# Small and large pieces of an attention batch put into halves over two steps, in a fused attention and Hadamard feed-forward kernel

## Chip, cores and metric

The kernel runs on one core of a Trainium2 chip. The metric is the device time of one execution in microseconds, lower being better. Three runs of the kernel before gave 2101.51, 2101.54 and 2102.27 us; the median is 2101.54 us.

## What is computed

Eight batches of 512 rows with 512 features, all float32. Attention has 16 heads of 32 features. Keys come from the row itself, queries and values from a compression to 128 features. Both are rotated (rotary embedding). Its output goes through an output projection and a layer norm and is added to the input; then a feed-forward block does the same with Hadamard transforms around its weights.

```python
x = layernorm(x_in)
c_kv = x @ W_dkv + b_dkv;  c_q = x @ W_dq + b_dq          # 512 -> 128
v = c_kv @ W_uv + b_uv                                     # 128 -> 512
q = rotary(c_q @ W_qr + b_qr);  k = rotary(x @ W_kr + b_kr)
attn = softmax(q @ k.T / sqrt(32)) @ v                     # 16 heads
x1 = x_in + layernorm(attn @ W_o + b_o)
h = fwht(layernorm(x1) * SU_ug) / 64
h = silu(h @ W_gate.T * s_g) * (h @ W_up.T * s_u)          # 512 -> 2048
out = x1 + layernorm((fwht(h * SU_dp) / 64) @ W_down.T * s_d)
```

The second Hadamard transform is applied to the down weights instead of the data ("fold"): its 16 parts are worked off during attention.

## The kernel before

**Two halves.** Attention takes the first 923 us or so, the feed-forward block the rest. The change touches attention alone.

**Steps.** Attention is one loop of 128 steps, written out by hand: the engines get their instructions in just the order of the program text, each engine its own queue. A batch has 4 groups of 4 heads, a group 4 steps (one for each 128 keys). Step "b.i" below is step i (0 to 15) of batch b; c is i modulo 4. Every step has the same core on TensorE (PE):

- `scores_t` (L564, L573): transposed scores t of 4 heads, first the rows' maxima as a bias in bf16, then k against q. They go to two PSUM tiles of two banks each, from a pool "s" of three.
- `weigh` (L606, "ops"): the weights of the step before times v.
- `row_max` (L527, "s"): scores of a group six steps ahead, into two more tiles of pool "s", from which VectorE (DVE) takes the maxima (L535, "nm").

So in a step pool "s" hands out t, t, s, s in turn. The second t of a step takes the tile that the first s of the step before had: it waits for DVE's first `nm`. The second s takes the first t's: it waits for ScalarE's (ACT) first exponential (L585, "p").

Some steps have more of it: at c = 2 the sums of the weights ("l", L623); at c = 3 the transposes of the maxima ("ps_b", L550), whose input GpSimd (POOL) makes by splitting the maxima into three bf16 parts (`split`, L543 to L545), issued two steps earlier, at c = 1. At c = 3 the second exponential stands behind the copy of ps_b (L554) in ACT's queue.

**Add-ups.** At c = 1 and c = 3 POOL adds two steps' weights (`add_up`, L594, four instructions, in place, so it must wait for `weigh`). At the next c = 0 DVE adds the two results (`add_pairs`, L599, two instructions), behind that step's `nm` in its queue.

**Pieces.** Everything else that attention needs is cut into pieces that stand in the steps. Large ones have four 512-column matmuls: `key` (L439), `compress` ("cq" and "ckv", L407), `out_proj` (L662). Small ones have one: `query` (L454), `value` (L466), `fold` (L485). `x_flip` (L394, "xt") is four transposes. Tables `BETWEEN` and `BEHIND` say which piece stands in which step: BETWEEN ahead of `row_max` (or, for steps in `TWO`, ahead of the BEHIND piece, with a tile of pool "s"), BEHIND at the end of the step. Pieces other than those of TWO use the one bank "f", which ACT must have emptied before the next one writes to it. In batches 1 to 5 the steps hold: 0 value and xt; 1 key and xt; 2 query; 3 value; 4 fold and xt; 5 compress; 6 key; 7 to 10 the four output projections, with a query at 8 and 9 and a fold at 10; 11 key; 12 query and compress; 13 value and xt; 14 key; 15 value.

**Behind a piece.** A key or a query leaves PSUM through ACT; its rotation follows (`rotate`): a shuffle on DVE (L420) and three POOL instructions (L421 to L423). Rotations wait in a list, `turns`; `turn()`, called twice in a step (ahead of `weigh` and behind `row_max`), issues all that wait. A fold is followed by four levels of adds on DVE (L493, L494, one level per step) and a store. x's row statistics, its normalization on ACT, its loads and the output's statistics stand in `early` and `later`, in steps of their own.

Of the kernel before, what the change touches and what calls it, by code (L numbers as in the profile page):

```python
# [10 lines left out]
F32 = mybir.dt.float32  # L11
BF16 = mybir.dt.bfloat16
I32 = mybir.dt.int32
AF = mybir.ActivationFunctionType
# [3 lines left out]
P = 128  # L18
NB, S, D = 8, 512, 512
DH, GH = 32, 4  # L20
NK = D // P
NT = S // P
# [11 lines left out]
def sandwich_kernel(  # L34
# [142 lines left out]
    def in_step(j, had, n):  # L177

        if had:
            in_had(j)  # L180
            if j + 2 < n:
                in_shift(j + 2)
            return
        in_flip(j)
        if j + 3 < n:
            in_load(j + 3)
        if j + 1 < n:
            in_norm(j + 1)
        if j + 2 < n:
            in_stats(j + 2)  # L190
# [51 lines left out]
    with ExitStack() as actx:  # L242
# [19 lines left out]
        def load_x(b, by=1):  # L262
            xs[b] = xpool.tile([P, NT, D], F32, tag="x", name=f"x{b}")
            xv = x[b].rearrange("(c p) d -> p c d", p=P)
            for c in range(0, NT, by):
                nc.sync.dma_start(out=xs[b][:, c : c + by, :], in_=xv[:, c : c + by, :])

        def load_row(b, t):

            if b < NB - 1:  # L270
                xr[b, t] = row.tile([P, D], F32, tag="xr", name=f"xr_{b}_{t}", bufs=2)
            else:
                xr[b, t] = fo.tile(
                    [P, D], F32, tag="wwza"[t], name=f"xr_{b}_{t}", bufs=2 - t // 2
                )
            nc.sync.dma_start(out=xr[b, t], in_=x[b, ts(t, P), :])

# [100 lines left out]
        def x_shift(b):  # L378
            mv, rs = stats[b]
            stats[b] = rs, shift_of(mv, rs, NT, f"x{b}")  # L380

        def x_norm(b, t):
            rs, sh = stats[b]
            xn[b, t] = row.tile([P, D], F32, tag="xn", name=f"xn_{b}_{t}", bufs=3)
            nc.scalar.activation(
                xn[b, t], xs[b][:, t, :], AF.Identity, bias=sh[:, t : t + 1], scale=rs[:, t : t + 1]
            )
# [26 lines left out]
        def rotate(dst, ps, bias, scale, name, first=None, second=None):  # L414
            lin = rp.tile([P, S], F32, tag="lin", name=f"lin_{name}")
            nc.scalar.activation(lin, ps, AF.Identity, bias=bias, scale=scale)

            def rest():
                rot = rp.tile([P, S], F32, tag="rot", name=f"rot_{name}", bufs=2)
                nc.vector.stream_shuffle(rot, lin, swap)  # L420
                (first or nc.gpsimd).tensor_mul(lin, lin, cs[:, 0, :])  # L421
                (second or nc.gpsimd).tensor_mul(rot, rot, cs[:, 1, :])
                (first or nc.gpsimd).tensor_add(dst, lin, rot)  # L423

            turns.append(rest)

        turns = []

        def turn():

            while turns:
                turns.pop(0)()

        def key(b, g, wide=False):
            if g == 0:
# [43 lines left out]
            )  # L479
            folds.append((n, w))  # L480

        def fold(n, wide=False):
            _, w = folds.pop(0)
            ps = bank(wide, f"fd_{n}").rearrange("p (c m) -> p c m", c=NI)
            nc.tensor.matmul(ps, lhsT=h128, rhs=w, start=True, stop=True)  # L485
            z = fo.tile([P, NI, NF], F32, tag="z", name=f"fz_{n}")
            a = fo.tile([P, NI, NF], F32, tag="a", name=f"fa_{n}")
            nc.scalar.copy(z, ps)

            def level(src, dst, h):  # L490
                sv = src.rearrange("p (a t b) n -> p a t (b n)", t=2, b=h)
                dv = dst.rearrange("p (a t b) n -> p a t (b n)", t=2, b=h)
                nc.vector.tensor_add(dv[:, :, 0, :], sv[:, :, 0, :], sv[:, :, 1, :])  # L493
                nc.vector.tensor_sub(dv[:, :, 1, :], sv[:, :, 0, :], sv[:, :, 1, :])  # L494

            def keep():
                nc.sync.dma_start(
                    out=wdd.rearrange("p (c m) -> p c m", c=NI)[:, :, ts(n, NF)], in_=w
                )

            levels.extend(
                [
                    lambda: level(z, a, 1),
                    lambda: level(a, z, 2),
                    lambda: level(z, a, 4),
                    lambda: level(a, w, 8),
                    keep,
                ]
            )

        levels = []


        brow, nms, pt, o_ps, o_sb, rec = {}, {}, {}, {}, {}, {}
# [245 lines left out]
        for t in range(3):  # L760
# [10 lines left out]

        BETWEEN = {
            0: (x_flip, 1, 1), 1: (x_flip, 1, 2), 4: (x_flip, 1, 3),
            8: (query, 1, 0), 9: (query, 1, 1), 12: (query, 1, 2), 13: (x_flip, 2, 0),
        }
        BEHIND = {
            0: (value, 0, 2), 1: (key, 0, 3), 2: (query, 0, 3), 3: (value, 0, 3),
            5: (compress, 1, "cq"), 6: (key, 1, 0), 7: (out_proj, -1, 0),  # L780
            8: (out_proj, -1, 1), 9: (out_proj, -1, 2), 10: (out_proj, -1, 3),
            11: (key, 1, 1), 12: (compress, 1, "ckv"), 13: (value, 1, 0), 14: (key, 1, 2),
            15: (value, 1, 1),
        }

        FIRST_BETWEEN = {i: p for i, p in BETWEEN.items() if i not in (8, 9)}
        FIRST_BEHIND = {
            **BEHIND, 7: (query, 1, 0), 8: (None, NB, None), 9: (key, 1, 1),
            10: (None, NB, None), 11: (query, 1, 1),
        }  # L790
        OUT = {7: 0, 8: 1, 9: 2, 10: 3}

        APART = {n: (0, 2) for n in range(NG - NK, NG - 2)}
        APART[NG - 2], APART[NG - 1] = (0, 2, 3), (0, 1, 2, 3)

        FOLDS = [4, 10, 15] + [NK * NT * b + i for b in range(1, NB - 1) for i in (4, 10)]
        FOLDS.append(NK * NT * (NB - 1) + 1)
        READ = [0] + [g - 3 for g in FOLDS[1:]]


        TWO = (8, 9, 10, 12, 15)

        def piece(table, b, i, wide=False):
            if b == 0 and table is BEHIND and i == 8:
                out_bias()
            pieces = table if b else FIRST_BETWEEN if table is BETWEEN else FIRST_BEHIND
            if i in pieces:
                fn, d, what = pieces[i]
                if 0 <= b + d < NB:
                    fn(b + d, what, *([True] if wide else []))  # L810
            at = NK * NT * b + i
            if at in FOLDS and (table is BETWEEN) == (b > 0 and i in TWO or i == 15 or b == NB - 1):
                fold(FOLDS.index(at), wide)
            if b == NB - 1 and (i, table is BEHIND) in ENTRY:
                in_step(*ENTRY[i, table is BEHIND], 2 * NT)

        places = [
            (0, False), (4, False), (4, True), (5, True), (6, True), (8, False), (10, False),  # L820
            (11, True), (12, False), (12, True), (13, True), (14, True), (15, True),
        ]
        ENTRY = {place: divmod(s, 2) for s, place in enumerate(places)}
        room["xin"] = lambda name: row.tile([P, D], F32, tag="xn", name=name, bufs=3)
# [9 lines left out]
        def early(b, i):  # L834

            if b > 0 and i - 3 in OUT:
                residual(b - 1, OUT[i - 3])
            if b + 2 < NB and i in (12, 14, 15):
                x_norm(b + 2, max(i - 13, 0))
            if i == 0 and 0 < b + 1 < NB:  # L840
                x_norm(b + 1, 3)

        def later(b, i):

            if b > 0 and i - 1 in OUT:
                out_stats(b - 1, OUT[i - 1])
            if b > 0 and i - 2 in OUT:
                out_shift(b - 1, OUT[i - 2])
            if b > 0 and i - 5 in OUT:
                store(b - 1, OUT[i - 5])  # L850
            if b + 2 < NB:
                if i == 4:
                    load_x(b + 2, NT)
                elif 6 <= i < 10:
                    x_stats(b + 2, i - 6)
                elif i == 11:
                    x_shift(b + 2)

        for t in range(NG * NT):
            n, c = divmod(t, NT)  # L860
# [4 lines left out]
            ends_group = c == NT - 1 and n + 1 < NG  # L865
            if not ends_group:
                second()
            turn()
            if c == 0 and n > 1:
                invert(n - 2)  # L870
            if c == 3 and n > 1:
                divide(n - 2)
            last_steps = t + AHEAD >= NG * NT
            if last_steps:
                piece(BETWEEN, b, i)
            if t > 0:
                weigh(*divmod(t - 1, NT))
            if ends_group:
# [6 lines left out]
                    sums(n - 1, APART[n - 1])  # L885
            elif c == 2 and n > 0:
                sums(n - 1)
            if not last_steps and (i not in TWO or b == NB - 1):
                piece(BETWEEN, b, i)
            if c == 0 and n > 0:  # L890
                weighed(n - 1)
            u = t + AHEAD
# [2 lines left out]
                if u % NT == NT - 1:  # L895
                    split(u // NT)
            early(b, i)
            turn()
            if c == 0 and 0 < n <= NG - NK:
                add_pairs(n - 1)  # L900
            later(b, i)
            if b == 0 and i == 6:
                out_bias_in()
            if levels and (c > 0 or 0 < i and b < 1):
                levels.pop(0)()
            if small:
                small.pop(0)()
            if t in READ:
                fold_load(READ.index(t))
# [14 lines left out]
                load_row(b, i - 12)  # L924
            elif b == NB - 1 and i in (8, 10):
                combine(*units[i // 2 - 4][1:])
            if i in TWO and b < NB - 1:
                piece(BETWEEN, b, i, True)
            piece(BEHIND, b, i)
            if n == NG - 1 and c == 2:  # L930
                invert(NG - 2)

# [682 lines left out]
```

## Time and profile before

| what | us |
|---|---|
| median of three runs | 2101.54 |
| the profiled execution | 2102.66 |
| its span, first to last instruction | 2100.9 |
| PE busy | 2076.8 |
| POOL busy | 1575.4 |
| DVE busy | 1414.4 |
| ACT busy | 745.3 |
| attention's batch 0 (46.78 to 148.89) | 102.11 |
| batch 4 (474.86 to 583.52) | 108.66 |
| first to last of batch 7's steps 0 to 14 (800.28 to 890.50) | 90.22 |

A step begins where the first bias matmul of `scores_t` starts (L564); times are counted from the span's start. A float32 matmul of one instruction in the program is two records in the trace: "x8" of a 512-column key are its four matmuls. In the timeline a row is a run of equal instructions with its start and the time to the end of its last one; as the next run starts before the last has drained, what a run costs is read from start to start. Granted clock was 1.00 in all stretches of attention.

### The profile page before, as it was taken

The numbers are of one execution on the slowest core, as the hardware profiler recorded it, in microseconds if no ns is written. First come the engines' busy times: TensorE is split into PE (matmuls) and PEld (weight loads), VectorE is DVE, ScalarE is ACT, GpSimd is POOL, SyncE is SP. The second block draws the span as 40 slices with busy tenths as digits, with TensorE's granted clock in tenths as the row PEclk, the third lists the DMA queues.
The fourth block names the chain that finished last, engine by engine and source line by source line (L and its number), as shares of the span: only waits on it lengthen the run. The fifth ranks groups of instructions, "written<-read, shape, count | busy, mean of one in ns | idle before, by whom it ended". The sixth has DMA issues, their size and how long they took to land.

```text
span 2100.9 us, 26741 instructions
## 1 busy us (share of the span) xinstructions
PE 2076.8 (99%) x9035; PEld 1057.4 (50%) x9042; DVE 1414.4 (67%) x2356; ACT 745.3 (35%) x1199; POOL 1575.4 (75%) x1629
## 2 busy tenths in 40 slices
PE   8999999999999999999999999999999999999998
PEld 4333333333333333344444677676676766777753
DVE  5698777676767677465545866678866678656542
ACT  3554545555555545522121122222222222222211
POOL 4787979787878889645453678788888879787852
PEclk9999999999999999999999999999999999999999
DMA  3112121212121122237454444444343344444432
GB/s 122 37 31 51 42 54 49 47 51 52 46 57 46 32 66 72 70 104 221 145 166 152 146 143 148 133 138 149 130 157 131 131 137 144 138 158 136 138 112 70
DMA packets 215913, 218.12 MB, mean 104 GB/s; under 512 B 87376, under 2 KB 147920, under 8 KB 215776
## 3 DMA queue, kind: packets, MB, share of 16 engines
q1 hardware_dynamic: 215424, 215.32, 33.2%
q8 instruction: 72, 1.18, 0.2%
q0 software_dynamic: 352, 1.08, 0.1%
q14 instruction: 65, 0.53, 0.1%
HBM read 169.18 MB, written 46.92 MB: 103 GB/s over the span
## 4 chain that ended last, share of the span: by engine, by line
PE 94%; DVE 3%; issue 1%; POOL 1%; ACT 1%; DMA 0%; SPq 0%; POOLq 0%; DVEq 0%; ACTq 0%
PE d L1123 24%; PE psy L1225 18%; PE s L527 6%; PE ops L606 6%; PE ps_k L439 5%; PE ps_y L662 5%; PE t L573 5%; PE u L1106 5%; PE g L1106 4%; PE psz L1516 3%; PE t L564 3%; PE l L623 2%; PE ps_q L454 2%; PE ps_v L466 1%; PE ps_cq L407 1%; PE fxh L207 1%
## 5 line engine op out<-in xcount | busy, mean ns | idle before, releaser
L1225 PE MATMUL psy<-wd,g 128*128 128x512 f32 x896 | 448.9, 592 | 0.0
L535 DVE TENSOR_REDUCE nm<-s 128x2 f32<-128x1024 f32 x256 | 300.8, 1216 | 175.1 <-PE s L527 175.1
L1347 POOL TENSOR_TENSOR pr<-pr,pr 128x512 f32<-128x512 f32 x294 | 391.6, 1357 | 9.0
L594 POOL TENSOR_TENSOR p<-p,p 128x512 f32<-128x512 f32 x244 | 330.2, 1384 | 22.1 <-PE ops L606 22.1
L585 ACT ACTIVATE p<-t 128x1024 f32<-128x1024 f32 x256 | 251.8, 1023 | 89.0 <-PE t L573 89.0
L1123 PE MATMUL d<-xb,wq 128*128 128x256 f32 x992 | 254.2, 380 | 1.9 <-DVE inner L1139 1.4
L1123 PEld LDWEIGHTS d<-tt,wq 128*128 128x128 f32 x864 | 164.0, 190 | 144.4 <-issue 106.0
L1123 PE MATMUL d<-tt,wq 128*128 128x256 f32 x864 | 233.8, 379 | 0.2 <-DVE pr L1144 0.2
L1140 POOL TENSOR_TENSOR pr<-inner 128x256 f32<-128x256 f32 x168 | 126.0, 750 | 138.5 <-DVE inner L1139 105.9
L1123 PEld LDWEIGHTS d<-xb,wq 128*128 128x128 f32 x992 | 186.7, 190 | 62.4 <-issue 30.1
L1225 PEld LDWEIGHTS psy<-wd,g 128*128 128x128 f32 x896 | 169.7, 190 | 49.3 <-issue 29.4
L1136 ACT COPY inner<-d 128x256 f32<-128x256 f32 x168 | 62.6, 373 | 309.6 <-PE d L1123 291.5
L1132 ACT COPY inner<-d 128x256 f32<-128x256 f32 x168 | 62.6, 372 | 300.3 <-PE d L1123 193.2
L527 PE MATMUL s<-kT,qT 32*128 32x512 f32 x1024 | 153.8, 639 | 0.7 <-DVE nm L535 0.7
L573 PE MATMUL t<-qT,kT 32*128 32x512 f32 x1024 | 142.8, 598 | 0.0
L606 PE MATMUL ops<-p,v 128*32 128x512 f32 x1024 | 136.8, 605 | 0.0
L1142 POOL TENSOR_TENSOR pr<-pr,inner 128x256 f32<-128x256 f32 x168 | 136.5, 813 | 0.0
L1123 PE MATMUL d<-T,wq 128*128 128x256 f32 x496 | 127.6, 380 | 0.2
L1144 DVE TENSOR_TENSOR pr<-d,inner 128x256 f32<-128x256 f32 x168 | 70.5, 420 | 75.5 <-PE d L1123 72.9
L439 PE MATMUL ps_k<-xT,wkr_sb 128*128 128x512 f32 x256 | 118.3, 605 | 0.7 <-ACT xT L397 0.7
L662 PE MATMUL ps_y<-wo_sb,oT 128*128 128x512 f32 x256 | 115.8, 593 | 0.9 <-DVE oT L657 0.6
L1135 DVE TENSOR_TENSOR inner<-d,inner 128x256 f32<-128x256 f32 x168 | 70.5, 419 | 62.4 <-PE d L1123 62.0
(219 smaller groups left out, 3263.8 us busy)
## 6 DMA issues: line engine op xcount, KB each, us to landing
wq<-wdeep SPq DMA_DIRECT2D x168, 448.0 KB, 4.2
wd<-wdd SPq DMA_DIRECT2D x112, 256.0 KB, 2.8
wdeep<-w SPq DMA_DIRECT2D x32, 448.0 KB, 5.5
xr<-in_x SPq DMA_DIRECT2D x32, 256.0 KB, 2.8
xin<-x1d SPq DMA_DIRECT2D x32, 256.0 KB, 4.0
xres<-x1d SPq DMA_DIRECT2D x32, 256.0 KB, 3.3
out<-fy SPq DMA_DIRECT2D x32, 256.0 KB, 2.0
rec<-rd SPq DMA_DIRECT2D x124, 64.0 KB, 2.0
```

The source lines that it names most:

```text
L439: nc.tensor.matmul(ps, lhsT=wkr_sb[:, k, ts(g, P)], rhs=xT[b][:, k, :], start=(k == 0), stop=(k == NK - 1),)
L527: nc.tensor.matmul(sp[j // 2][:, j % 2, :], lhsT=qT[b][rows, g, ts(qc, P)], rhs=kT[b][rows, g, :], start=True, stop=True,)
L535: nc.vector.tensor_reduce(nms[n][:, qc, 2 * h : 2 * h + 2], sp[h], AX.X, ALU.max, negate=True)
L573: nc.tensor.matmul(sp[j // 2][:, j % 2, :], lhsT=kT[b][rows, g, ts(c, P)], rhs=qT[b][rows, g, :], start=False, stop=True,)
L585: nc.scalar.activation(pt[n, c, h], sp[h], AF.Exp)
L594: nc.gpsimd.tensor_add(into, into, pt[n, c, j // 2][:, j % 2, :])
L606: nc.tensor.matmul(o_ps[n][j * DH : (j + 1) * DH, :], lhsT=vv[b][:, c, ds(g * P + j * DH, DH)], rhs=pt[n, c, j // 2][:, j % 2, :], start=( ...
L662: nc.tensor.matmul(ps, lhsT=oT[b][:, k, ts(qc, P)], rhs=wo_sb[:, k, :], start=False, stop=(k == NK - 1),)
L1106: nc.tensor.matmul(ps, lhsT=w[:, SLOT[n], k, :], rhs=rhs[:, k, :], start=k == 0, stop=k == 1)
L1123: nc.tensor.matmul(ps, lhsT=w[:, INNER[m]], rhs=rhs[m], start=True, stop=True)
L1225: nc.tensor.matmul(ys_[t], lhsT=g[:, ts(t, P)], rhs=w, start=n == 0, stop=n == NI - 1)
L1347: nc.gpsimd.tensor_add(pr[n][:, h], pr[a][:, h], pr[b][:, h])
```

## The change

The tables are replaced by a plan of (step, place) to pieces, with three places: "between" (ahead of `row_max`, bank "f"), "beside" (ahead of the piece at the end, a tile of pool "s") and "behind" (the end, bank "f").

- Most pairs of a small and a large piece are put in halves over two steps (`both`, `halves`, `half`): in each step 256 columns of the small and 256 of the large one share bank "f", side by side, and leave it by two ACT instructions. After the second half the rotation or the fold's levels follow.
- The four values of the next batch stand beside the four output projections (steps 7 to 10). Queries and folds are no longer there.
- x's transposes move from steps 0, 1, 4 and 13 to 8, 9, 12 and 13; its loads, statistics and normalizations move with them, and so do the reads of the folds' weights.
- `turn(True)` issues one rotation at a time instead of all that wait.
- A level of a fold and a part of the output bias no longer fall into the same step, and no level falls into c = 0 (but for the last batch).
- Pieces move to earlier steps across the batches: all keys and queries of batch 1 stand in batch 0 now (one of each stood in batch 1), and batch 7's last key, last query and last two values, which stood in its own steps 0 to 3, stand in batch 6. Batch 7 has two folds (steps 3 and 8) instead of one (step 1).

In batches 1 to 5 the steps then hold: 1 and 2 query with key; 3 and 4 query with ckv; 5 and 6 fold with key; 7 to 10 value and output projection; 11 and 12, 13 and 14 query with key; 15 and the next batch's 0 fold with cq.

```diff
-        BETWEEN = {
-            0: (x_flip, 1, 1), 1: (x_flip, 1, 2), 4: (x_flip, 1, 3),
-            8: (query, 1, 0), 9: (query, 1, 1), 12: (query, 1, 2), 13: (x_flip, 2, 0),
-        }
-        BEHIND = {
-            0: (value, 0, 2), 1: (key, 0, 3), 2: (query, 0, 3), 3: (value, 0, 3),
-            5: (compress, 1, "cq"), 6: (key, 1, 0), 7: (out_proj, -1, 0),
-            8: (out_proj, -1, 1), 9: (out_proj, -1, 2), 10: (out_proj, -1, 3),
-            11: (key, 1, 1), 12: (compress, 1, "ckv"), 13: (value, 1, 0), 14: (key, 1, 2),
-            15: (value, 1, 1),
-        }
...
-        FOLDS = [4, 10, 15] + [NK * NT * b + i for b in range(1, NB - 1) for i in (4, 10)]
-        FOLDS.append(NK * NT * (NB - 1) + 1)
-        TWO = (8, 9, 10, 12, 15)
...
+        def both(b, i, small_, large):
...
+            if large and small_:
+                for h in range(2):
+                    put(b, i + h, "behind", halves, 0, h, small_, large)
+            elif small_:
+                put(b, i, "behind", *small_)
+
+        def halves(_, h, small_, large):
+            ps = bank(False, f"ps_{large[0].__name__}_{large[1]}_{large[2]}_{h}")
+            both_ = [(*small_, None, None)[:3], large]
+            for leave in [half(h, ps[:, ts(n, HC)], *which) for n, which in enumerate(both_)]:
+                leave()
+
+        both(0, 0, (value, 0, 2), (key, 0, 3))
+        put(0, 2, "behind", query, 0, 3)
+        put(0, 3, "behind", value, 0, 3)
+        both(0, 4, (fold,), (compress, 1, "cq"))
+        both(0, 6, (query, 1, 0), (key, 1, 0))
+        put(0, 8, "behind", out_bias)
+        both(0, 9, (query, 1, 1), (key, 1, 1))
+        put(0, 11, "beside", query, 1, 2)
+        put(0, 11, "behind", compress, 1, "ckv")
+        both(0, 12, (value, 1, 0), (key, 1, 2))
+        put(0, 14, "beside", query, 1, 3)
+        put(0, 14, "behind", key, 1, 3)
+        for t in range(3):
+            put(0, 15 + t, "beside", value, 1, t + 1)
+        both(0, 15, (fold,), (compress, 2, "cq"))
+        for t, i in enumerate((0, 1, 4)):
+            put(0, i, "between", x_flip, 1, t + 1)
+        for t, i in enumerate((9, 12, 13, 16)):
+            put(0, i, "between", x_flip, 2, t)
+        for b in range(1, NB):
+            both(b, 1, (query, b + 1, 0), (key, b + 1, 0))
+            both(b, 3, (query, b + 1, 1), (compress, b + 1, "ckv"))
+            if b < NB - 1:
+                both(b, 5, (fold,), (key, b + 1, 1))
+            for t in range(NT):
+                put(b, 7 + t, "beside", value, b + 1, t)
+                put(b, 7 + t, "behind", out_proj, b - 1, t)
+            both(b, 11, (query, b + 1, 2), (key, b + 1, 2))
+            both(b, 13, (query, b + 1, 3), (key, b + 1, 3))
+            if b < NB - 1:
+                both(b, 15, (fold,), (compress, b + 2, "cq"))
+            for t, i in enumerate((8, 9, 12, 13)):
+                put(b, i, "between", x_flip, b + 2, t)
+        put(NB - 1, 3, "behind", fold)
+        put(NB - 1, 8, "beside", fold)
...
+        READ = [1]
+        for b in range(NB - 1):
+            READ += [NK * NT * b + 12, NK * NT * (b + 1) + 2]
+        READ[-1] = NK * NT * (NB - 1)
+        READ.append(NK * NT * (NB - 1) + 4)
...
+        NORMS = [(8, 11, 12, 14), (7, 8, 9, 11)]
+        STATS = [(3, 4, 5, 6), (1, 2, 3, 5)]
...
-            turn()
+            turn(True)
...
-            if levels and (c > 0 or 0 < i and b < 1):
+            busy_dve = False
+            if levels and (c > 0 or b == NB - 1):
+                busy_dve = len(levels) % 5 != 1
                 levels.pop(0)()
-            if small:
+            if small and not busy_dve:
                 small.pop(0)()
```

The half of a query, as an example of `half`, which does the same for values, folds, keys and compressions:

```python
            if fn is query:
...
                if h == 0:
                    split_in_two["q"] = rp.tile([P, S], F32, tag="lin", name=f"lin_q{b}_{what}")
                dst = split_in_two["q"]
                nc.tensor.matmul(
                    ps, lhsT=wqr_sb[:, ts(what, P)], rhs=cT[b, "cq"][:, cols], start=True, stop=True
                )

                def leave():
                    nc.scalar.activation(
                        dst[:, cols], ps, AF.Identity, bias=bqs[:, what : what + 1], scale=QSCALE
                    )
                    if h == 1:
                        rotation(qT[b][:, what, :], dst, f"q{b}_{what}")
```

## Prediction

> **What bounds it now.** I read the page first, then busy time stretch by stretch, then PE's and POOL's timelines of one batch. The page gives the bound:
>
> ```profile
> span 2100.9 us, 26741 instructions
> ...
> PE 2076.8 (99%) x9035; PEld 1057.4 (50%) x9042; DVE 1414.4 (67%) x2356; ACT 745.3 (35%) x1199; POOL 1575.4 (75%) x1629
> ```
>
> PE is hardly ever without an instruction, so only shorter or fewer matmuls, or waits hidden inside "busy", can be saved. Busy time by batch (stretch, length, then PE, PEld, DVE, ACT and POOL busy):
>
> ```profile
> 46.78:148.89 102.11, 98.49 (x575) 32.83 (x575) 79.74 (x97) 52.94 (x68) 82.45 (x79) 1.00 0.13 30
> ...
> 474.86:583.52 108.66, 108.61 (x616) 37.15 (x617) 78.91 (x102) 57.79 (x77) 90.48 (x91) 1.00 0.20 50
> ...
> 800.28:890.50 90.22, 87.00 (x545) 28.40 (x544) 55.10 (x90) 49.84 (x66) 71.11 (x89) 1.00 0.26 69
> ```
>
> POOL is busy 90.5 of batch 4's 108.7 us, so it has 18 us to spare in a batch, and its queue is the second thing to watch. PE's hidden waits show from start to start. Two steps of batch 4, the first behind a large piece, the second behind a small one:
>
> ```profile
> 487.86 0.40 PE L564 MATMUL t<-brow,ones_b 32*128 32x512 bf16 x4
> 488.08 1.03 PE L573 MATMUL t<-qT,kT 32*128 32x512 f32 x8
> 489.04 1.06 PE L606 MATMUL ops<-p,v 128*32 128x512 f32 x8
> ...
> 497.98 0.71 PE L564 MATMUL t<-brow,ones_b 32*128 32x512 bf16 x4
> 498.31 1.24 PE L573 MATMUL t<-qT,kT 32*128 32x512 f32 x8
> 499.48 1.07 PE L606 MATMUL ops<-p,v 128*32 128x512 f32 x8
> ```
>
> t costs 489.04 - 487.86 = 1.18 us, or 1.50 where its second tile still waits for DVE's `nm`: 0.32 lost. Such light steps are followed by this six times in a batch (1.9 us). With waits of 0.15 to 0.26 us of s for an exponential (four) and 0.22 of a query beside a projection, PE loses about 3 us of a batch. Batch 4 without waits would take 105.6. Its parts, start to start: t 1.18, ops 1.00, s 1.07 (3.25 a step), sums 0.85, ps_b 0.33, xt 0.58, a small piece 1.06, a large one 3.64. By the same parts batch 0 has some 94 us of work and 8 of waits, and batch 7 to the feed-forward block 7 of waits. All of attention: 8 + 6 x 3.05 + 7 = 33.5 us of waits, the most that this change could gain.
>
> **The change, part by part.**
>
> *Halves on PE.* In the feed-forward block four 256-column records take 0.215 us each (1499.83 to 1500.69), two of 512 columns 0.43 each (1500.69 to 1501.55): halving is free but for what each piece pays at its start, 0.03 us a pair, 0.2 a batch, 1.5 in all. ACT empties a pair of halves by two instructions of 0.37 (the page's 128x256 copies) to some 0.47 us, instead of one of 0.59 to 0.69; ACT is busy 57.8 of 108.7, and its next exponential comes 1.3 us into the step. Nothing.
>
> *Light steps gone.* A pair of halves is 2.36 us at the end of a step, instead of 1.06. s is in DVE 1.17 us after it starts, and the first `nm` takes 1.2; the next t then starts 3.4 us behind s: in time. -1.9 us a batch, -0.2 for the query.
>
> *Values beside the projections.* At step 7 (c = 3) the value's tile of pool "s" is that of the second exponential, which stands behind the copy of ps_b. In batch 3 that exponential ended at 446.26, 4.1 us into step 11; the value would start at 3.25 + 0.33 = 3.6. +0.6 us a batch, new. The same pattern stood once in batch 0, where a fold waited for ACT at 146.98.
>
> *x's transposes.* They are 0.58 us wherever they stand. In a step without xt, sums or ps_b the second s waits 0.15 to 0.26 for an exponential: steps 5, 8, 9, 12 before, 0, 1, 4, 5 after. No difference.
>
> *SP's queue.* x's load (from step 4 to 14) and the folds' reads (to 2 and 12) pass the transfers for the reciprocals. Those land in 2.0 us and are used three steps later (some 17 us). Nothing.
>
> *POOL's queue, the main term.* POOL's work stays the same, but moves: eight rotations of a batch now fall two by two into steps 13, 15 and 3, and one each into 5 and 7, all in or just behind the stretch of light steps from 11 to 6, which also gets shorter. What POOL pays, each row a run of its queue (start, length):
>
> ```profile
> 472.17 1.72 POOL L421 TENSOR_TENSOR lin_k<-lin_k,cs 128x512 f32<-128x512 f32 x1
> 473.85 1.27 POOL L422 TENSOR_TENSOR rot_k<-rot_k,cs 128x512 f32<-128x512 f32 x1
> ...
> 482.76 5.98 POOL L594 TENSOR_TENSOR p<-p,p 128x512 f32<-128x512 f32 x4 [1.03 <-PE ops L606]
> ...
> 490.09 1.28 POOL L421 TENSOR_TENSOR lin_k<-lin_k,cs 128x512 f32<-128x512 f32 x1
> ...
> 499.31 4.96 POOL L594 TENSOR_TENSOR p<-p,p 128x512 f32<-128x512 f32 x4
> ```
>
> A rotation is 3.85 us (490.09 to 493.94), an add-up 4.96; beside one of DVE's `add_pairs` (481.39 to 483.95) it took 5.98, and a rotation's first instruction beside DVE's division took 1.72 instead of 1.27. So each `add_pairs` instruction costs POOL about 1.1 us, a division 0.45, a level of a fold 0.35 (add-ups of 5.31).
>
> Count from step 13 to the split in step 5, whose result the transposes in step 7 need. POOL can start 3.4 us into step 13 (behind DVE's `add_pairs` of step 12 and the shuffle). Work: 7 rotations x 3.85 = 27.0, 5 add-ups x 4.96 = 24.8, 3 splits x 1.4 = 4.2, a residual 1.2: 57.2. Slowed by DVE: 4 `add_pairs` instructions 4.4, two divisions 0.9, three levels 1.0: 6.3. Done at 66.9. PE, with no wait, comes to those transposes at 6.2 + 6.5 + 5.9 + 5.8 + 5.8 + 6.5 + 5.9 + 5.8 + 5.8 + 6.5 (steps 13 to 6) + 2.2 = 62.9. **PE is held up 4 us a batch**, and 1.3 more if POOL once runs dry: I take 4.8. The lower bound is 0 (POOL slowed by nothing: done at 60.6), the upper 8 (DVE's adds also wait, see below). Part of it falls earlier: the add-up of step 15 ends 28 to 29 us into this count, DVE's `add_pairs` in step 0 waits for it until 30 to 32, `nm` of step 1 stands behind it in DVE's queue, ready since 28, and t of step 2 waits for `nm`: 1.4 to 2.7 us. What is queued behind POOL's late split is ps_b, the second exponential and the value.
> The kernel before has slack here: its split of step 13 ended at 471.04, with transposes due at 472.4. Where it had none, PE waited for POOL already:
>
> ```profile
> 144.98 0.40 PE L550 MATMUL ps_b<-ident_b,parts 128*128 128x128 bf16 x4 [0.68 <-POOL parts L545]
> ```
>
> [...]
>
> *Batches 0 and 7.* Batch 0 gets about 6 us of PE work more, batch 7 loses 6.8 (three small pieces and a key). Batch 7 doesn't get shorter by it: in its steps 0 to 6 DVE has seven `nm` pairs (16.5), six levels of folds instead of four (11.4), the feed-forward block's input (9.3), `add_pairs` and the rest (3.6): 40.8, one behind the other, against 33 us of PE work; the same steps took 41.2 before. So DVE bounds there, PE's waits go from 7 to about 14. In batch 0 the work fills waits: from 8 to about 6 (its first steps' 1.8 stay, two queries beside at c = 3 cost 0.6 each).
>
> *Sum.* PE's work +1.5. Waits: batch 0 6, batch 1 3 (its rotations were issued over longer steps), batches 2 to 6 3.05 - 1.9 - 0.2 + 0.6 + 0.1 + 4.8 = 6.5 each, batch 7 14: 55.5 against 33.5. **+23.5 us**: 2102.66 + 23.5 = 2126.2 by the profiled execution, which stood 1.1 above the median; so **2125 us** beside 2101.5.
>
> **Rivals.**
>
> 1. *POOL keeps up* (0.25). If the queue isn't slowed by DVE, 60.6 comes ahead of 62.9, and only the gains are left: batches 2 to 6 lose 1.7 instead of 3.05 (-6.7), batch 0 -2.3, batch 1 -1, batch 7 +5, work +1.5: about -3.5; with batch 7's DVE no worse than before, -8.5. Time 2093 to 2098. For it: POOL is idle 18 us in a batch. Against it: it is idle in steps 7 to 10 now, where rotations no longer come. It decides at 2.3 us of slowing in the count; the rows give 6.3. This is the case on the other side.
> 2. *The two queues wait for each other* (0.13). Late `add_pairs` push DVE's levels and shuffles behind them, so that rotations start later too: 8 us a batch, 5 x 3.2 more: 2141.
> 3. *A draw* (0.12). Waits of 1.5 us a batch by POOL and a batch 7 as before: within 4 us of 2101.
>
> **Numbers.** The forecast (2125, 2112 to 2136 on its own) has 0.50, the rivals 0.25, 0.13 and 0.12. A difference of 0.2% (4.2 us) is about what a measurement can tell from none. Rival 1 holds both -8.5 (0.18, faster) and -3.5 (0.07, no change). Faster 0.18, same 0.19, slower 0.63. The range takes in most of rival 1 and rival 2: 2095 to 2142.
>
> **What would show it.** Right: batches 2 to 6 at 111 to 114 us; ps_b waiting for POOL's split in step 7; DVE's `add_pairs` of step 0 waiting for POOL's add-up; t no longer at 1.50 behind halves; POOL without a gap from step 13 to 7. Batch 7's steps 0 to 6 at 41 to 45 us with DVE full. Wrong: a batch at 107 us or less, POOL idle in steps 14 or 2, or pairs of halves that take more than 2.4 us.

## The result, and the profile after

The changed kernel takes 2131.17 us (median of four runs, 2130.36 to 2134.39) beside 2101.74 for the kernel before (four runs, 2101.51 to 2102.27): a ratio of 1.0143 [1.0125, 1.0160], slower by 29 us. The forecast was 2125, its range 2095 to 2142. The profiled execution took 2131.31, its span 2129.5.

The page first: the span, the busy times, and the chain of work that ended last, by engine.

```profile
span 2129.5 us, 27677 instructions
...
PE 2077.3 (98%) x9450; PEld 1134.2 (53%) x9452; DVE 1401.7 (66%) x2356; ACT 757.9 (36%) x1281; POOL 1571.8 (74%) x1629
...
PE 76%; POOL 13%; DVE 7%; issue 2%; ACT 1%; DMA 0%; POOLq 0%; SPq 0%; DVEq 0%; ACTq 0%
```

PE has the same busy time as before (2076.8) in a longer span, and the chain no longer runs through PE almost alone. Before, it was

```profile
PE 94%; DVE 3%; issue 1%; POOL 1%; ACT 1%; DMA 0%; SPq 0%; POOLq 0%; DVEq 0%; ACTq 0%
```

Busy time by batch (stretch, length, then PE, PEld, DVE, ACT, POOL, granted clock):

```profile
150.97:263.14 112.17, 109.75 (x686) 49.13 (x686) 77.44 (x103) 61.33 (x91) 82.30 (x86) 1.00 0.19 48
488.35:600.98 112.63, 109.16 (x678) 48.62 (x678) 77.49 (x102) 59.67 (x88) 90.26 (x91) 0.98 0.19 47
...
823.19:870.24 47.05, 36.82 (x250) 11.36 (x250) 38.70 (x50) 21.33 (x28) 40.04 (x45) 0.93 0.34 80
```

The rows are batch 1, batch 4 and the steps 0 to 6 of batch 7. Steps 0 to 6 of batch 7 before were

```profile
800.28:841.49 41.21, 39.62 (x259) 12.34 (x259) 31.92 (x44) 22.80 (x30) 37.72 (x41) 1.00 0.27 72
```

In batch 4 PE's busy time is 3.5 us less than the stretch, where it was 0.05 before; and the granted clock, 1.00 in all stretches before, is 0.98 there and 0.93 in batch 7. From the starts of the steps, the 28.6 us between the two spans are

| where | before | after | difference |
|---|---|---|---|
| up to batch 0 | 46.78 | 45.75 | -1.0 |
| batch 0 | 102.11 | 105.22 | +3.1 |
| batch 1 | 108.63 | 112.17 | +3.5 |
| batches 2 to 5, each | 108.67 | 112.62 | +3.95, four times 15.8 |
| batch 6 | 108.09 | 109.57 | +1.5 |
| batch 7, steps 0 to 6 | 41.21 | 47.05 | +5.8 |
| batch 7, steps 7 to 14 | 49.03 | 48.20 | -0.8 |
| from there to the end | 1210.4 | 1211.1 | +0.7 |

In a batch from 2 to 5 two steps alone are longer than their parts: step 2 takes 8.29 us instead of 6.47, step 7 takes 11.97 instead of 8.28. Step 7 of batch 3 in PE's timeline (start, length, line, the idle time ahead of it and what ended it):

```profile
420.94 1.06 PE L688 MATMUL ops<-p,v 128*32 128x512 f32 x8
423.85 0.40 PE L632 MATMUL ps_b<-ident_b,parts 128*128 128x128 bf16 x4 [1.84 <-POOL parts L627]
424.18 1.52 PE L609 MATMUL s<-kT,qT 32*128 32x512 f32 x8
425.85 2.08 PE L471 MATMUL ps_v<-wuv_sb,ckv 128*128 128x512 f32 x2 [0.15 <-ACT p L667]
```

and the busy times of the stretch behind it:

```profile
424.81:428.23 3.42, 3.27 (x12) 1.08 (x5) 3.20 (x6) 1.96 (x4) 2.50 (x3) 0.50 0.00 0
```

The transposes wait 1.84 us for POOL's split, as forecast. What was not forecast: for the next 3.42 us the granted clock is 0.50, and the value's matmuls, 1.12 us elsewhere, take 2.08. Of the 3.69 us that step 7 has too much, 1.84 is POOL's, 0.15 the value's wait, and 1.7 the clock. Step 2 of batch 4 shows the other wait (DVE, POOL and PE in one timeline):

```profile
498.31 1.27 POOL L424 TENSOR_TENSOR lin_k<-lin_k,cs 128x512 f32<-128x512 f32 x1
498.38 2.27 DVE L681 TENSOR_TENSOR p<-p,p 128x1024 f32<-128x1024 f32 x1 [1.16 <-POOL p L676]
499.53 2.24 POOL L425 TENSOR_TENSOR rot_k<-rot_k,cs 128x512 f32<-128x512 f32 x1
...
500.58 2.34 DVE L617 TENSOR_REDUCE nm<-s 128x2 f32<-128x1024 f32 x2
501.84 0.39 PE L646 MATMUL t<-brow,ones_b 32*128 32x512 bf16 x2 [1.44 <-DVE nm L617]
```

DVE's second `add_pairs` of step 0 begins only when POOL's add-up of step 15 is done; the maxima (`nm`) stand behind it, and t of step 2 waits 1.44 us for them. In batch 7 the same chain is longer:

```profile
828.90 5.93 POOL L676 TENSOR_TENSOR p<-p,p 128x512 f32<-128x512 f32 x4
...
834.87 2.27 DVE L681 TENSOR_TENSOR p<-p,p 128x1024 f32<-128x1024 f32 x1 [1.15 <-POOL p L676]
...
837.06 1.48 DVE L501 TENSOR_TENSOR fa<-fz 128x256 f32<-128x256 f32 x1
...
839.86 2.34 DVE L617 TENSOR_REDUCE nm<-s 128x2 f32<-128x1024 f32 x2
...
841.12 0.61 PE L646 MATMUL t<-brow,ones_b 32*128 32x512 bf16 x2 [7.23 <-DVE nm L617]
```

The add-up of step 15 starts at 828.90, 5.7 us into batch 7, behind two rotations of step 15. PE is idle for 7.23 us, and then runs at half clock until 844.65: step 2 of batch 7 takes 14.72 us.

### The profile page after: what moved, and what is told of

It is laid out like the page before. It is cut to its first block, busy times and chain, and to the rows that moved or that the text cites. A ratio compares the mean times of both kernels' runs of the same rounds, so it can differ in the third digit from the quotient of the medians.

```text
span 2129.5 us, 27677 instructions
## 1 busy us (share of the span) xinstructions
PE 2077.3 (98%) x9450; PEld 1134.2 (53%) x9452; DVE 1401.7 (66%) x2356; ACT 757.9 (36%) x1281; POOL 1571.8 (74%) x1629
## 3 DMA queue, kind: packets, MB, share of 16 engines
q0 software_dynamic: 352, 1.08, 0.1%
## 4 chain that ended last, share of the span: by engine, by line
PE 76%; POOL 13%; DVE 7%; issue 2%; ACT 1%; DMA 0%; POOLq 0%; SPq 0%; DVEq 0%; ACTq 0%
PE d L1243 23%; PE psy L1345 18%; POOL p L676 6%; PE ps_y L744 5%; PE g L1226 5%; PE u L1226 5%; PE s L609 3%; PE ops L688 3%; PE psz L1636 3%; PE t L655 2%; DVE nm L617 2%; PE ps_v L471 2%; POOL lin_q L424 1%; POOL rot_q L425 1%; DVE p L681 1%
## 5 line engine op out<-in xcount | busy, mean ns | idle before, releaser
L676 POOL TENSOR_TENSOR p<-p,p 128x512 f32<-128x512 f32 x244 | 316.4, 1329 | 31.9 <-PE ops L688 21.1
L655 PE MATMUL t<-qT,kT 32*128 32x512 f32 x1024 | 136.8, 595 | 0.0
L1280 DVE SCALAR_TENSOR_TENSOR g<-pr,wsu 128x512 f32<-128x512 f32 x96 | 109.5, 1142 | 3.2 <-POOL pr L1467 3.2
```

Of the source, the lines that this page charges most:

```text
L655: nc.tensor.matmul(sp[j // 2][:, j % 2, :], lhsT=kT[b][rows, g, ts(c, P)], rhs=qT[b][rows, g, :], start=False, stop=True,)
L676: nc.gpsimd.tensor_add(into, into, pt[n, c, j // 2][:, j % 2, :])
```

## The experiments

Theory: POOL's queue. The rotations, bunched in steps 13, 15 and 3, hold up its add-ups and splits. Rivals: the plan costs PE or ACT time by itself (halves, values beside the projections), or DVE bounds. All ratios are to the kernel before, run on the same chip.

**Even turns.** The rotations are spread out. The fourth buffer that this takes gets its room from a table of the feed-forward block, which is loaded later for it (those lines are not shown; from the last step of attention to the end both kernels take 1211.1 us).

```diff
-            turn(True)
+            if b == 0 or c % 2 == 0:
+                turn(True)
...
             early(b, i)
-            turn(True)
+            if b == 0:
+                turn(True)
...
-        rp = actx.enter_context(tc.tile_pool(name="a_rope", bufs=3))
+        rp = actx.enter_context(tc.tile_pool(name="a_rope", bufs=4))
```

> The changed kernel with one thing altered: from batch 1 on a rotation is turned only in even steps (c = 0 and 2), one in each, so that it never stands in GpSimd's queue ahead of an add-up or a split of an odd step. The four rotations that then wait at once need a fourth buffer for their inputs; its room comes from the feed-forward block's scale row, which is loaded where that block begins. All is computed. Theory (GpSimd's queue is late because the rotations are bunched in steps 13, 15 and 3): steps 2 and 7 go back from 8.29 and 11.97 us to 6.5 and 8.3 to 8.9, no stretch at half clock in batches 2 to 5, these batches 107.1 to 107.9 us, batch 1 about 109.3, batch 6 about 106; batch 7's steps 0 to 6 at 41 to 46. Sum 2131 - 4 x 5 - 3 - 3 - (1 to 6): 2099 to 2104. Rival A (the plan itself is bad: halves, or the value beside the projection, cost the time, and GpSimd is only named because it is last): 2120 to 2131, with step 7 held by something else. Rival B (GpSimd has too much work wherever it stands): 2110 to 2125, with ps_b waiting for a split in other steps.

2103.84 us, ratio 1.0009 [1.0000, 1.0019]: 27 us back. Busy time by batch (1, 4, and batch 7's steps 0 to 6):

```profile
150.76:260.69 109.93, 109.40 (x685) 49.14 (x686) 77.13 (x99) 61.32 (x91) 80.36 (x86) 1.00 0.20 49
476.07:583.76 107.69, 107.16 (x678) 48.01 (x679) 77.31 (x102) 59.72 (x88) 88.28 (x91) 1.00 0.20 50
...
797.41:842.25 44.84, 36.73 (x250) 11.03 (x250) 39.54 (x54) 21.31 (x28) 42.01 (x47) 0.96 0.34 79
```

Step 2 is back at 6.47, step 7 at 8.89, the clock at 1.00 in batch 4. The order of POOL's queue was the cause in batches 2 to 5, and not the amount of its work, which has hardly changed (88.28 us busy instead of 90.26). Batch 4 is 0.97 us shorter than in the kernel before. Step 7's last 0.6 is the value:

```profile
520.75 1.14 PE L609 MATMUL s<-kT,qT 32*128 32x512 f32 x8
522.42 1.12 PE L471 MATMUL ps_v<-wuv_sb,ckv 128*128 128x512 f32 x2 [0.53 <-ACT p L667]
```

**Thinner rotations.** The changed kernel, the two multiplications left out in batches 2 to 7.

```diff
-                (first or nc.gpsimd).tensor_mul(lin, lin, cs[:, 0, :])
-                (second or nc.gpsimd).tensor_mul(rot, rot, cs[:, 1, :])
+                if name[:2] in ("q0", "k0", "q1", "k1"):
+                    (first or nc.gpsimd).tensor_mul(lin, lin, cs[:, 0, :])
+                    (second or nc.gpsimd).tensor_mul(rot, rot, cs[:, 1, :])
```

> The changed kernel, and the rotations of batches 2 to 7 leave out their two multiplications on GpSimd (the cosine and the sine are not applied; only the addition is left): 8 x 2.55 = 20 us of GpSimd's work less in a batch from batch 1 on, PE's, ScalarE's and DVE's instructions unchanged. Theory (GpSimd's queue): the waits of steps 2 and 7 go, batches 2 to 5 at 107.1 to 107.9, batch 7's step 2 falls from 14.7 to under 9, the whole at 2096 to 2104. Rival A (DVE or the plan bounds): 2120 to 2131.

2099.35 us, ratio 0.9989 [0.9979, 0.9998]. Batches 2 to 5 take 107.72, as with even turns, though POOL has 65.9 us of work there instead of 88.3: once its queue is not late, less of its work gains nothing. Batch 7's steps 0 to 6 take 42.89 instead of 47.05. Its step 2 takes 10.55, not under 9: t still waits 2.50 us there, and some 6.8 us at half clock follow (the granted clock of steps 0 to 6 is 0.92).

**Nothing halved**, beside even turns.

```diff
             if large and small_:
-                for h in range(2):
-                    put(b, i + h, "behind", halves, 0, h, small_, large)
+                put(b, i, "behind", *small_)
+                put(b, i + 1, "behind", *large)
```

> The run before, but nothing is halved: the small piece stands whole in the first step of a pair, the large one whole in the second. All is computed, all else stands where it stood. Theory (halving itself is nearly free on PE and ACT, and pays by keeping t from waiting for DVE in light steps, 0.32 us in each): six light steps a batch come back, 1.9 us a batch, 10 to 13 us above the run with even turns: 2110 to 2117 where that one takes 2099 to 2104. Rival (halving costs more than its 0.03 us a pair, in PE or in ScalarE's extra instructions): 5 to 15 us below the run with even turns.

2110.91 us, ratio 1.0043 [1.0028, 1.0058]: 7.1 us above even turns, so halving gains. Batch 4 takes 108.72 instead of 107.69: 1.03 us, not 1.9. Steps 0 and 1 take 7.27 + 4.57 whole and 5.79 + 5.87 halved. Halved, t costs 1.18 instead of 1.50 behind the small piece; but s, from its start to the next piece, costs 1.25 and 1.33 us where it was 1.13 and 1.33, and 1.07 where it does not wait: 0.18 us remain in these two steps. By pair of steps the gain is from 0.02 (1 and 2) to 0.30 us (11 and 12).

**TensorE kept busy** in step 7 of batches 2 to 5 of the changed kernel.

```diff
+        def stay(m):
+            ps = ps_f.tile([P, S], F32, tag="f", name="stay")
+            for _ in range(m):
+                nc.tensor.matmul(ps, lhsT=ones_b, rhs=bo3, start=True, stop=True)
+
         def bias_rows(n):
+            if n % NK == 2 and 2 <= n // NK <= 5:
+                stay(9)
```

> The changed kernel, with nine matmuls of 512 columns in bf16 (about 0.215 us each, 1.9 us in all, their result is not used) ahead of the transposes in step 7 of batches 2 to 5, where TensorE otherwise is idle for 2.0 us and the granted clock then is 0.5 for 3.4 us. All is computed. Theory (the idle time itself brings the clock down): step 7 at 10.3 us instead of 11.97, granted clock 1.00 all through batches 2 to 5, the whole 6 to 7 us shorter: 2124 to 2126. Rival (the clock falls for another reason, or the dummies only push the split's consumers back): 2131 or up to 8 us more.

2128.30 us, ratio 1.0127 [1.0112, 1.0142], 2.9 below the changed kernel (6 to 7 were expected). The granted clock is 0.997 over the whole run, where it was 0.994, and the value's matmuls in step 7 of batch 4 take 1.12 us instead of 2.08: without the idle time the clock does not fall there. But step 7 is at 11.05, not 10.3 (PE's timeline, batch 4):

```profile
532.02 2.12 PE L632 MATMUL stay<-bo,ones_b 128*128 128x512 bf16 x9
534.19 0.38 PE L639 MATMUL ps_b<-ident_b,parts 128*128 128x128 bf16 x4
534.50 1.14 PE L609 MATMUL s<-kT,qT 32*128 32x512 f32 x8
536.18 1.12 PE L471 MATMUL ps_v<-wuv_sb,ckv 128*128 128x512 f32 x2 [0.53 <-ACT p L674]
```

The dummies took 2.12 us for a wait of 1.84, and at full clock the value waits 0.53 for the exponential, which the half clock had hidden but for 0.15. So the clock's 1.7 us were worth 1.7 - 0.38 = 1.3 net, 0.28 of which went to the dummies: 0.9 to 1.0 a batch, as measured (11.97 to 11.05).

**A late split**, on even turns: extra multiplications ahead of the split of step 5.

```diff
+            late = {2: 4.5, 3: 5, 4: 5.5, 5: 6.5}.get(n // NK, 0) if n % NK == 2 else 0
+            if late:
+                scratch = rp.tile([P, S], F32, tag="rot", name=f"late_{n}", bufs=2)
+                for j in range(math.ceil(late)):
+                    cols = slice(0, S if j + 1 <= late else S // 2)
+                    nc.gpsimd.tensor_mul(scratch[:, cols], cs[:, 0, cols], cs[:, 1, cols])
             m, rest = parts[n % 2], nms[n]
```

> The run with even turns, with extra multiplications on GpSimd (their result is not used) ahead of the split in step 5 of batches 2, 3, 4 and 5: 4.5, 5, 5.5 and 6.5 of 128x512, each 1.27 us. All is computed. In the run with even turns that split ends 4.7 us ahead of its transposes. Theory: TensorE waits in step 7 for what is over 4.7 us, so 1.1, 1.65, 2.4 and 3.6 us; the granted clock falls to half for a stretch of 3.41 us where more than about half of such a stretch was idle, so surely in batch 5, mostly in batch 4, perhaps in batch 3, not in batch 2. Batch 2 1 us longer than 107.7, batch 5 3.6 and up to 1.7 more. Rival (lateness of a split is taken up by the value's wait for the exponential or elsewhere): under half of that.

One run, 2118.86 us, so its time has no interval. ps_b waited 1.30, 1.86, 2.65 and 4.00 us in batches 2 to 5; step 7 took 10.25, 10.81, 13.30 and 14.59 instead of 8.89. The batches:

```profile
261.62:370.68 109.06, 107.23 (x678) 48.02 (x678) 77.77 (x102) 59.76 (x88) 93.31 (x95) 1.00 0.19 48
370.68:480.30 109.62, 107.23 (x679) 48.02 (x679) 78.78 (x102) 59.76 (x88) 95.62 (x96) 1.00 0.20 52
480.30:592.40 112.10, 108.92 (x678) 48.59 (x678) 77.06 (x102) 59.83 (x88) 95.51 (x97) 0.98 0.19 48
592.40:705.79 113.39, 109.39 (x677) 48.73 (x677) 77.07 (x102) 59.83 (x88) 96.80 (x98) 0.97 0.16 40
```

A microsecond of lateness beyond the slack costs a microsecond of PE: the extra work ahead of the split lasted 6.27 us in batch 2 and 6.80 in batch 3 (0.53 more), the waits differ by 0.56. The first two cost just their waits; with 2.65 and 4.00 us about 1.7 us come on top, for the clock (0.50 from 529.52 to 532.94 and from 638.75 to 645.58).

**Values moved** from steps 7 to 10 to steps 8, 9, 10 and 12, on even turns.

```diff
-                put(b, 7 + t, "beside", value, b + 1, t)
+                put(b, (8, 9, 10, 12)[t], "beside", value, b + 1, t)
```

> The run with even turns, and the four values beside pieces go to steps 8, 9, 10 and 12 instead of 7 to 10. All is computed. Theory (at c = 3 the value waits for the second exponential, which stands behind the copy of ps_b): step 7 falls from 8.89 to 7.2 (the wait of 0.6 and the value's own 1.06 gone), step 12 rises by 1.06, a batch 107.1 instead of 107.7, the whole 3.6 us below the run with even turns (2103.8): 2100. Rival (the 0.6 is ScalarE's time and comes back at the next step): 2103 to 2104.

2098.79 us, ratio 0.9984 [0.9975, 0.9993], 5.0 below even turns. A batch takes 107.01 instead of 107.69: step 7 lost 1.55 (8.89 to 7.34), step 12 gained 0.86. That is 0.68 a batch; over batches 1 to 6 the starts of the steps differ by 4.2.

**A fold moved** from batch 7 to batch 6, on even turns, and then with the values moved as well.

```diff
-        put(NB - 1, 3, "behind", fold)
+        put(NB - 2, 12, "between", fold)
...
-        READ[-1] = NK * NT * (NB - 1)
+        READ[-2:] = NK * NT * (NB - 2) + 7, NK * NT * (NB - 2) + 13
...
-            if levels and (c > 0 or b == NB - 1):
+            if levels and (c > 0 or b >= NB - 2):
```

> The run with even turns, and the fold of batch 7's step 3 is done in batch 6's step 12 (its weights are read in step 7, those of the next in step 13, and in batch 6 a level is also put on DVE in steps with c = 0). All is computed. Theory (DVE bounds batch 7's first steps, where six levels of folds stand, 41 us of its work): with four levels there, steps 0 to 6 fall from 44.8 to 41 to 42.5, batch 6 grows by 1 (the fold's matmul), the whole 1 to 3 us below the run with even turns: 2101 to 2103. Rival (GpSimd's rotations that are left for batch 7 bound there): no change in steps 2 and 3 (9.1 and 7.7), 2104 to 2105.

> Even turns, the values in steps 8, 9, 10 and 12, and the fold moved to batch 6: the two edits before it together. All is computed. Theory: the two gains add up, 5 to 7 us below the run with even turns, 2097 to 2099: 0.1 to 0.2% faster than the kernel before. Rival (one wait takes the place of the other): 2100 to 2104.

2107.50 us, ratio 1.0027 [1.0016, 1.0037], and 2101.89, ratio 1.0001 [0.9992, 1.0009]: both worse than without it. The edit did not do what it was meant for. Batch 7's steps 0 to 6 hold five levels with it and five without it: the moved fold's last level now falls into step 0,

```profile
803.56 0.49 DVE L501 TENSOR_TENSOR fw<-fa 128x256 f32<-128x256 f32 x1
803.98 1.50 DVE L502 TENSOR_TENSOR fw<-fa 128x256 f32<-128x256 f32 x1
```

and with even turns alone the fold of step 3 had only its first level there. These steps take 44.80 where they took 44.84 (the granted clock of the whole run is 0.996, where it was 0.998), and 46.04 where they took 44.09 with the values moved; batch 6 got 4.8 us longer (110.80), PE idle for 1.91 us in its step 14 while DVE's maxima were late. Whether the number of levels bounds batch 7 was not tested.

**The feed-forward block's input** in its steps of before: on the changed kernel alone, and on even turns with the values moved.

```diff
-            (0, False), (1, True), (2, True), (4, False), (4, True), (5, True), (6, True),
-            (8, False), (11, True), (12, True), (13, True), (14, True), (15, True),
+            (0, False), (4, False), (4, True), (5, True), (6, True), (8, False), (10, False),
+            (11, True), (12, False), (12, True), (13, True), (14, True), (15, True),
```

> The changed kernel, with only the feed-forward block's input of batch 7 back in the steps that it had before. All is computed. Theory: batch 7's steps 0 to 6 take 47.0 us, of which two causes share the 5.8 us over the kernel before; the input's two pieces are worth 2 to 4 of them: 43 to 45 there, the whole at 2127 to 2129.5. If GpSimd's rotations of batch 6's end alone make it, no change: 2131.

> Even turns, the values in steps 8, 9, 10 and 12, and in batch 7 the feed-forward block's input goes back to the steps that it had in the kernel before (two of its pieces to steps 10 and 12 instead of 1 and 2). All is computed. Theory (in batch 7's first steps TensorE waits for DVE, 44.1 us in steps 0 to 6, because the change put two more pieces of the input there, with some 3 us of DVE's work, and the transposes of step 3 wait for a bank that DVE empties late): steps 0 to 6 at 40 to 42, steps 10 and 12 longer by 0.6 to 1.1 each, the whole 1 to 3 us below the run with the values moved (2098.8): 2096 to 2098. Rival (GpSimd and DVE hand over to each other there whatever the input does): 2098 to 2100, with steps 1 to 3 as they were.

2131.14 us, ratio 1.0140 [1.0127, 1.0154], and 2099.25, ratio 0.9982 [0.9973, 0.9991]: nothing gained by either. On the changed kernel steps 0 to 6 of batch 7 went from 47.05 to 46.14, and steps 7 to 14 gave more than that back; step 2 takes 14.54 as before. So the input's place is not the cause.

**One rotation earlier, at the end of batch 6**, on the second of these; and then three of them.

```diff
-            if b == 0 or c % 2 == 0:
+            if b == 0 or c % 2 == 0 and t != NK * NT * (NB - 1):
                 turn(True)
...
-            if b == 0:
+            if b == 0 or t == NK * NT * (NB - 1) - 1:
                 turn(True)
```

The second, instead of these lines:

```diff
-            if b == 0:
+            if b == 0 or b == NB - 2 and i in (7, 9, 13):
                 turn(True)
```

> The run before, and the rotation that fell into step 0 of batch 7 is turned at the end of step 15 of batch 6. All is computed. Theory (DVE's add_pairs in step 0 of batch 7 takes 4.25 us instead of about 2.5 because a rotation stands beside it on GpSimd, and the maxima behind it are late): step 1 or 2 of batch 7 1 to 2 us shorter, the whole 1 to 2 us below the run before. Rival (GpSimd is as busy there with the add-up, which the rotation now delays): no change or 1 us more.

> Even turns, the values in steps 8, 9, 10 and 12, the feed-forward block's input in its steps of before, and in batch 6 three rotations more in odd steps (7, 9 and 13, behind the add-up), so that no rotation is left for the add_pairs in step 0 of batch 7. All is computed. In the run that turned one at the end of step 15, that rotation still began only when the add-up of step 15 was done, beside add_pairs, which took 3.50 us for two; and the maxima behind it made TensorE idle for 2.71 us in step 2. Theory (GpSimd's rotation slows add_pairs, and add_pairs makes the maxima late): add_pairs 2.3 to 2.8, the idle time in step 2 down to 1.6 to 2.0, so that the clock falls there seldom; the whole at 2094 to 2096. Rival (what DVE has in those steps by itself makes the wait): 2.5 to 2.7 us of idle time as before, 2095 to 2099.

2095.71 us, ratio 0.9972 [0.9960, 0.9983], and 2096.93, ratio 0.9977 [0.9968, 0.9986]. The first is the shortest of all, but not for the reason given. Step 2 of batch 7 without and with the edit, in the windows of the two kernels:

```profile
803.38:812.11 8.73, 6.02 (x40) 1.53 (x38) 6.79 (x9) 2.52 (x3) 8.36 (x13) 0.80 0.01 2
```

```profile
801.87:808.96 7.09, 4.38 (x40) 1.35 (x38) 6.82 (x9) 2.52 (x3) 7.01 (x7) 1.00 0.01 2
```

Without the clock they are the same step: PE idle 2.71 us in both, waiting for `nm` (step 1 takes 5.14 in both). Only the granted clock differs, 0.80 and 1.00. The rotation began at 797.34 behind the add-up of step 15 and ran beside `add_pairs` all the same: its theory falls. In the second of them another rotation (a query's) came into step 0 instead, `add_pairs` took 3.69 us, and PE was idle for 3.96: the edit did not do what it was meant for. Steps 0 to 6 differ by 3.6 us between the first pair (43.88 and 40.27): 1.64 are the clock's in step 2, 2.5 stand in step 4, where PE was idle for 2.08 us and for 1.17; the granted clock of the whole runs is 0.997 and 0.999. The runs of either scatter over 4 us (2095.7 to 2099.7 and 2094.4 to 2098.9). How much of the 3.5 us between 2099.25 and 2095.71 is the edit's stays open.

## Why the prediction was right, and where it was not

*POOL's queue, the main term: right in mechanism, and in the sum partly by luck.* Forecast: 4.8 us a batch. Between the changed kernel and even turns, batch 4 differs by 112.63 - 107.69 = 4.9. But the waits are 1.44 for t in step 2 (forecast 1.4 to 2.7, the step 1.82 longer) and 1.84 for ps_b in step 7 (forecast the rest, 2.1 to 3.4); the other 1.3 is the clock, which the prediction left out. So the waits were over-estimated, and the clock made up for it. From step 13 of batches 2, 3 and 4 to step 7 of the next POOL's queue had no gap over 0.3 us but for 3.2 us at the start of step 13 and 0.64 us in step 3, much as forecast (3.4 us, and dry at most once). The chain by way of `add_pairs` and `nm` is as written.

*Batches 2 to 6.* 6.5 us of waits against 3.05 were forecast, +17.3 in all; measured 4 x 3.95 + 1.5 = +17.3. Batches 2 to 5 at 112.6 lie within the 111 to 114, batch 6 at 109.57 does not: that the total agrees is chance.

*Halving.* "-1.9 a batch" was mis-sized: 1.03 in the run with nothing halved. What failed is "No difference" for the waits of s: some halved steps bring them back (1.25 us instead of 1.13 in step 0).

*Value beside the projection.* "+0.6 us a batch": 0.53 of wait at full clock, 0.68 gained by moving it.

*Batch 1.* "its rotations were issued over longer steps", hence no change: +3.5. Even turns gives 2.2 of it back (112.17 to 109.93), so POOL was late there too. The rest is work: two values of batch 1 stand in its own steps 0 and 1, and one of x's transposes in step 0 (7.05 and 6.73 instead of 5.79 and 5.87, 2.1 us), less the gain of 1 that every batch has. The sum had no such term.

*Batch 7, the step that failed.* "DVE bounds there", 41 to 45 us "with DVE full": 47.05, with DVE busy for 38.70 of them; and before it was busy for 31.92 of 41.21. Five levels fell into these steps, not six. Two pieces of the input fewer took off 0.9; thinner rotations took off 4.2, even turns 2.2. It was POOL again: the two rotations of step 15 ahead of the add-up, then `add_pairs` and `nm`; and 6.8 us at half clock behind the idle time. What holds t up for 2.7 us with even turns and the input elsewhere is not settled: `add_pairs`, still beside a rotation, and levels are ahead of `nm`, and no run took `add_pairs` out of a rotation's way.

*Batch 0*: +4 forecast with what stands before it, +2.1 measured; no run shows why. The sum, +23.5, was 5 short of 28.6: batches 1 and 7 brought 8.3 us more than forecast (+3.5 for 0, +5.0 for +0.2), all else 3 less. The range, 2095 to 2142, would have held a gain as well, so the time alone says little; the waits in steps 2 and 7 say more.

*The rivals.* With its rotations thinned, and so not all computed, POOL keeps up, and the time is 2099.35, near rival 1's 2093 to 2098. Even turns, with all computed, reach 2103.84, a draw; with the values moved as well the plan is 0.16% faster than the kernel before, and 0.28% is the best seen. So the gain that was expected of the plan is there, some 1 us a batch; the late queue, with the clock, took five times that. Rival 2, where the two queues wait for each other, asked for 8 us a batch; batches 2 to 5 lost 4.9.

## What to carry over

When pieces are moved, follow the order of every in-order queue that serves them, and not only its busy share: POOL was busy for 80 to 82% of a batch both with and without the 27 us of loss. Put work that can wait (a rotation that is needed a group later) behind work that somebody waits for, one piece to a gap; here that cost one more buffer. And count for a wait of TensorE not only itself: here one of 1.84 us had 3.42 us at half clock behind it, which cost 1.7 us more, while one of 1.44 us had none.

## What the runs showed of the hardware

In the runs looked at here the granted clock changed at times that lie whole multiples of 3.4133 us apart. In the changed kernel's run it fell to 0.50 in attention at 312.18, 424.82, 537.46, 650.09 and 837.83 us, four times for 3.413 us and the last time for 6.827; from the first to the second are 112.64 us, 33 times 3.4133, and from the first to the last 525.65, 154 times. The kernel before has two changes in its run, at 6.87 and 2095.83 us, 612 times 3.4133 apart. With a late split the falls at 529.52 and 638.75 us are 32 times apart. So each run's changes lie on a grid (a field is the stretch between two of its lines), and half clock in attention lasted one or two fields: one cost 1.7 us in step 7 and 1.64 in step 2 of batch 7.

Put on that grid, PE's idle time sorts the fields of the kernel before and of the changed kernel. In attention the changed kernel's four fields with 1.84 to 1.87 us of it and the two with 3.41 and 3.29 (834.42 to 841.24) were followed by one at half clock, and so was, at the end of each run, the field in which PE's work ends (2.66 and 2.52 us); a field with 1.48 us or less never was. With a late split a field with 1.78 us (413.47 to 416.88, PE busy for 1.63 of 3.41) was not. Whether idle time alone decides was not shown. The length of a wait does not: in step 2 of batch 7 a wait of 2.71 us had 3.42 us at 0.50 behind it (807.29 to 810.71), and with one rotation earlier a wait of 2.71 us left the clock at 1.00 (801.87 to 808.96).

Some of DVE's and POOL's instructions took longer beside each other, on either side. In the changed kernel an `add_pairs` instruction took some 1.2 us in 32 records and 2.3 in 21, all of these beside POOL's work. In the rows of step 2 above a POOL multiplication ran until 499.57, `add_pairs`, started at 498.38, ended 1.08 us later at 500.65, and the next multiplication, started at 499.53, ended 1.12 us after that, at 501.77 (2.24 us instead of 1.27). The second instruction of a level (L502) took 0.42 us in the 5 records with no work of POOL beside it; of the 59 beside such work 35 took 1.48 to 1.51 us, and 22 no more than 0.45.
